# Layer 1's state-space scan in units of 32 channels by 4 states: shared delta and delta*u tiles, B and C spread by TensorE, the product with C in place

## The chip, the cores and the metric

The kernel runs on one core of one Trainium2 chip. The metric is the device time of one execution in microseconds (us); lower is better. Three runs of the kernel before gave 7250.67, 7251.33 and 7258.51 us, median 7251.33 us.

## What is computed

Four layers run in sequence on an image tensor of 4 x 96 channels x 64 x 64, in float32. Layer 0 is two Mamba blocks over the 4096 tokens of each image. Layer 1, which the change is about, is two 2-D selective scans ("ss2d", a and b). Layers 2 and 3 (a spectral block, quantized feed-forwards, linear attention) are untouched. The core of layer 1, for each image and each of four directions k (rows, columns, and both backwards), with d = 96 channels, N = 8 states, L = 4096 tokens:

```
x_dbl = jnp.einsum('bkdl,kcd->bkcl', xs, xproj_w)
dts = jnp.einsum('bkrl,kdr->bkdl', x_dbl[:, :, :R], dt_w)
Bs = x_dbl[:, :, R:R + N]
Cs = x_dbl[:, :, R + N:]
A = -jnp.exp(A_logs).reshape(K, d, N)
delta = jax.nn.softplus(dts + dt_b[None, :, :, None])
dA = jnp.exp(delta[..., None] * A[None, :, :, None, :])
dBu = delta[..., None] * jnp.transpose(Bs, (0, 1, 3, 2))[:, :, None] * xs[..., None]
...
h = a * h + bu
return (h, jnp.einsum('bkdn,bkn->bkd', h, c))
```

Around the scan stand a 3x3 depthwise convolution with Silu in front, a gate branch Silu(z), and behind it a sum of the four directions, a layer norm, the gate and an output projection.

## The kernel before

Three stages follow each other: `stage_mamba` (layer 0), `stage_ss2d` (layer 1) and `stage_tokens` (layers 2 and 3). Within a stage nothing is issued directly: each operation is recorded by `Plan.add`, and `Plan.order` (L388) then lists all of them engine by engine, by costs that it assumes for each kind of operation, the order of recording breaking ties. So every instruction of a stage carries line 474 in the profile, and rows are told apart by tile names. The five engines' queues run in that order, each waiting for what its next instruction needs; all DMAs are issued by SyncE (SP), in order. `Plan(close_first=True)` (layer 0 only) makes the plan finish a "mm" tile of PSUM that it has opened before it opens another.

**Layer 1.** There are 8 blocks (4 images, a and b). A block has 16 **turns**: 4 directions (two forwards, two backwards) by 4 tiles of T = 1024 tokens. `Tokens.prepare` makes delta (96 rows; 16 more rows of the same matmul hold B and C), writes both to DRAM (`dd`), multiplies delta by the input on POOL (`du`) and writes 32 of its 96 rows to DRAM (`ud`). `narrow` reads the 8 rows of C back, splits them into three bf16 parts (`split_steps`) and stacks them (`bc_stack`, 24 rows). `mix` makes the turn's table `bc`: B is spread over the 128 partitions by a DMA, C by two bf16 matmuls and two ScalarE copies.

A turn has 6 **units** of 16 channels by 8 states on 128 partitions (`Scan`, L589). For each unit, at its step s:

- `load` (5 units ahead): a 512 KB DMA spreads 16 rows of delta over 128 partitions (`sc_d`).
- `decay` (2 ahead): ScalarE makes exp(A * delta).
- the input term delta*u*B. In 4 units of 6 ("spread"), `inputs` has TensorE spread delta*u into PSUM (`s<-du,c_sel`, two float32 matmuls) and `scan` has VectorE multiply it there by B. In the other 2, a 512 KB DMA spreads `ud` (`sc_u`) and POOL multiplies it by B; the decay is then in PSUM.
- `scan`: VectorE's `tensor_tensor_scan` over 1024 tokens, backwards through a reversed view where the direction is backwards; ScalarE keeps the last column (`carry`) for the next turn.
- `outputs`: POOL multiplies the states by C into a new tile `sc_h`.
- `reduce`, after each round of three units: TensorE sums over the states into `y` in PSUM (`y<-sc_h,c_red`), and `end` adds that to `ysum` on VectorE after two rounds.

`plan` (L1510) interleaves the next turns' `prepare`, `narrow` and `mix`, and over a whole block the work for its neighbours: the next block's convolution (`mm<-xp,w_conv`, 9 float32 matmuls for each 512 tokens) and gates, and the previous block's `finish`.

**Layer 0** already has the form that the change gives to layer 1 (`QuadScan`, L755): units of 32 channels by 4 states, so that one `sc_d` and one `sc_u` tile serve several units; TensorE spreads B from the bf16 stack into PSUM (`s<-bc_stack,selb`); VectorE multiplies that by `sc_u`; POOL multiplies the states `sc_h` by C into a second tile `sc_y`. Both layers have 768 units.

Of the kernel before, what the change touches and what calls it, by code (L numbers as in the profile page):

```python
# [11 lines left out]
F32 = mybir.dt.float32  # L12
# [21 lines left out]
def in_psum(index):  # L34

    return index % 3 != 2


def shape_constants():
# [12 lines left out]
    red = np.zeros((128, 32), f)  # L52
    red[p, p // QS] = 1.0
    out["c_red0"] = red
    red = np.zeros((128, 2, 32), f)
    for r in range(2):
        red[p, r, r * 16 + p // NS1] = 1.0
    out["c_red1"] = red
    at = np.arange(3 * NS0) % NS0
    sel = [at[:, None] == QS * q + p % QS for q in range(NS0 // QS)]  # L60
    out["c_selb0"] = np.stack(sel, 1).astype(f)
    out["c_selbc"] = (np.arange(3 * NS1)[:, None] % NS1 == p % NS1).astype(f)
    sel = np.zeros((C, C // 16, 128), f)
    for j in range(C // 16):
        sel[j * 16 + p // NS1, j, p] = 1.0
    out["c_sel1"] = sel
# [28 lines left out]
def arrange(w):  # L95
# [36 lines left out]
    def blocks(a):  # L132
# [30 lines left out]
        [w[q + "A_logs" + x].reshape(NDIR, C * NS1 // 128, 128) for x in s], 0  # L163
    ).transpose(3, 0, 1, 2)
# [400 lines left out]
class Turn:  # L565
# [4 lines left out]
    def in_psum(self, index):  # L570
        return in_psum(index)

    def begin(self, q, yps):

        return False


class Unit:


    def __init__(self, turn, q, r, j, index, rows):
        self.turn, self.q, self.r, self.j, self.index, self.rows = turn, q, r, j, index, rows
        self.spread = turn.in_psum(index)
        self.first = index == 0
        self.round = []
        self.last = False


class Scan:  # L589

    LOOK = 5

    def __init__(self, k, rep, ps, n_state, red, bufs):
        self.k = k  # L600
        self.rep, self.ps, self.red, self.bufs = rep, ps, red, bufs
        self.ns, self.dl = n_state, 128 // n_state
        self.per = 32 // self.dl
        self.yps = None

    @property
    def nc(self):
        return self.k.nc

    def spread_states(self, src):  # L610

        return bass.AP(src.tensor, src.offset, [(T, self.ns), (0, self.dl), (1, T)])

    def spread_channels(self, src, j):

        at = src.offset + j * self.dl * T
        if self.ns == NS0:
            return bass.AP(src.tensor, at, [(0, self.ns), (T, self.dl), (1, T)])
        return bass.AP(src.tensor, at, [(T, self.dl), (0, self.ns), (1, T)])

    def units(self, turn, parts):


        out = []
        for q, groups in enumerate(parts):
            for r in range(self.per):
                new = []
                for g, rows in groups:
                    new.append(Unit(turn, q, r, g * self.per + r, len(out) + len(new), rows))
                    new[-1].round = new  # L630
                out += new
            out[-1].last = True
        return out

    def load(self, u):
        nc = self.nc
        u.d = self.rep.tile([128, T], F32, tag="sc_d", name="sc_d", bufs=self.bufs[0])
        nc.sync.dma_start(out=u.d, in_=self.spread_channels(u.turn.dd, u.j))
        if not u.spread:
            u.u = self.rep.tile([128, T], F32, tag="sc_u", name="sc_u", bufs=self.bufs[1])  # L640
            nc.sync.dma_start(out=u.u, in_=self.spread_channels(u.turn.ud, u.j))

    def decay(self, u):
        if not u.spread:
            u.s = self.ps.tile([128, T], F32, tag="s", name="s_ps", bufs=2)
            self.nc.scalar.activation(u.s, u.d, AF.Exp, scale=u.turn.acol(u.j))
        else:
            self.nc.scalar.activation(u.d, u.d, AF.Exp, scale=u.turn.acol(u.j))

    def inputs(self, u):  # L650
        u.s = self.ps.tile([128, T], F32, tag="s", name="s_ps", bufs=2)
        with self.nc.side_by_side(overlap=25.0 if self.halves(u) else 0.0):
            for h, (table, du) in enumerate(u.turn.spread(u)):
                self.nc.tensor.matmul(u.s[:, h * W:(h + 1) * W], table, du, start=True, stop=True)

    def halves(self, u):

        return u.turn.spread(u)[0][1].ap[0][1] <= 64

    def scan(self, u):  # L660
        nc = self.nc
        init, keep = u.turn.carries(u.j)
        if not u.spread:
            a, b, u.h = u.s, u.u, u.u
        else:
            a, b, u.h = u.d, u.s, u.d
            nc.vector.tensor_tensor(b, b, u.turn.bc[:, 0, :], ALU.mult)
        if u.turn.rev:
            nc.vector.tensor_tensor_scan(u.h[:, ::-1], a[:, ::-1], b[:, ::-1], init, ALU.mult, ALU.add)
        else:  # L670
            nc.vector.tensor_tensor_scan(u.h, a, b, init, ALU.mult, ALU.add)
        if keep is not None:
            nc.scalar.copy(keep, u.h[:, 0:1] if u.turn.rev else u.h[:, T - 1:T])

    def outputs(self, u):
        u.c = self.rep.tile([128, T], F32, tag="sc_h", name="sc_h", bufs=self.bufs[2])
        self.nc.gpsimd.tensor_tensor(u.c, u.h, u.turn.bc[:, 1, :], ALU.mult)

    def reduce(self, us):

        nc = self.nc
        r = us[0].r
        held = True
        if r == 0:
            self.yps = self.ps.tile([128, T], F32, tag="y", name="y_ps", bufs=1)
            held = us[0].turn.begin(us[0].q, self.yps)
        halves = [[h] for h in range(T // W)] if len(us) > 2 else [range(T // W)]
        for hs in halves:
            with nc.side_by_side():
                for h in hs:  # L690
                    for u in us:
                        row, col, at = u.rows[h]
                        nc.tensor.matmul(
                            self.yps[row:row + 32, col:col + W], self.red[:, r, :], u.c[:, at:at + W],
                            start=not held, stop=r == self.per - 1, skip_group_check=True,
                        )

    def run(self, units, plan):


        nc = self.nc
        works = []
        for s in range(-self.LOOK, len(units) + 5):
            def at(n):
                return units[n] if 0 <= n < len(units) else None

            works += plan(s)
            u = at(s + self.LOOK)
            if u:
                if u.first:  # L710
                    u.turn.ready.finish()
                self.load(u)
            for w in works:
                w.pace(s)
            works = [w for w in works if not w.done]
            u = at(s - 3)
            if u and u is u.round[-1]:
                self.reduce(u.round)
            u = at(s - 4)
            if u and u.last:  # L720
                u.turn.end(u.q, self.yps)
            u = at(s + 2)
            if u and u.spread:
                self.decay(u)
            u = at(s)
            if u:
                self.scan(u)
            u = at(s + 2)
            if u:
                if not u.spread:  # L730
                    self.decay(u)
                else:
                    self.inputs(u)
            if u and not u.spread:
                nc.gpsimd.tensor_tensor(u.u, u.u, u.turn.bc[:, 0, :], ALU.mult)
            u = at(s)
            if u:
                self.outputs(u)
        for w in works:
            w.finish()  # L740


class Quad:
# [11 lines left out]
class QuadScan:  # L755
# [4 lines left out]

    LOOK = 4

    def __init__(self, k, rep, ps, red, selb, bufs, y):
        self.k = k
        self.rep, self.ps, self.red, self.selb, self.bufs, self.y = rep, ps, red, selb, bufs, y
        self.yps = None
# [5 lines left out]
    def units(self, turn, parts):  # L772
# [3 lines left out]
        for m, (rows, rounds) in enumerate(parts):  # L776
            for r, those in enumerate(rounds):
                new = []
                for g, q, pooled in those:
                    new.append(Quad(turn, m, g, q, pooled, len(out) + len(new), rows[g]))  # L780
                    new[-1].round, new[-1].place = new, (r, len(rounds))
                out += new
            out[-1].last = True
# [18 lines left out]

    def load(self, u):
        def fill(tag, bufs, src):
            t = self.rep.tile([128, T], F32, tag=tag, name=tag, bufs=bufs)
            self.nc.sync.dma_start(out=t, in_=src)
            return t
# [63 lines left out]
    def run(self, units, plan):  # L871
# [4 lines left out]
        for s in range(-self.LOOK, len(units) + 5):  # L876
# [9 lines left out]
            for w in works:  # L886
                w.pace(s)
# [1040 lines left out]
```

## Time and profile before

One execution was profiled: 7245.79 us, of which the span from the first to the last instruction is 7243.7 us. "Busy" is the time in which an engine has an instruction at work.

| | span of 7243.7 us | layer 0, 104 to 2790 us | layer 1, 2850 to 6062 us |
|---|---|---|---|
| length, us | 7243.7 | 2686 | 3212 |
| PE (TensorE) busy, us | 6069.7 | 2164.0 | 2793.8 |
| DVE (VectorE) busy, us | 5862.6 | 2513.7 | 2708.2 |
| ACT (ScalarE) busy, us | 4424.7 | 1567.3 | 2269.8 |
| POOL (GpSimd) busy, us | 5855.0 | 2530.9 | 2821.8 |
| mean busy share of the 16 DMA engines | 0.60 | 0.42 | 0.91 |
| granted TensorE clock | 0.865 | 0.81 | 0.92 |

A busy share near 1 does not by itself name the bound: an engine that is in step with another has to wait for it now and then, and what a stage can gain is read from the idle time of its busiest engine and from what that idle time waited for.

### The profile page before, as it was taken

The page shows a single profiled execution, that of the slowest core. Times are in us where ns is not written, and L with a number is a line of the kernel's source. Part 1 is how long each engine was busy: PE and PEld are TensorE (multiplying, and loading weights), DVE is VectorE, ACT ScalarE, POOL GpSimd, SP SyncE. Part 2 cuts the span into 40 slices and gives each one's busy share as a digit, 9 for nine tenths or more (in the row PEclk, how much of TensorE's full clock was granted, in tenths as well). Part 3 has the DMA queues.
Part 4 walks back from the last instruction along what each step waited for, and adds up shares of the span by engine and source line. Part 5 has one row for each costly group of instructions (what it writes and reads, how often), then busy time and mean ns, then how long its engine had stood idle before and what let it go on. Part 6 is the DMA issues. An engine that isn't in the chain of part 4 may idle for free. (4 is left out here: it accounts for less than half of the span.)

```text
span 7243.7 us, 79973 instructions
## 1 busy us (share of the span) xinstructions
PE 6069.7 (84%) x26408; PEld 2258.7 (31%) x26408; DVE 5862.6 (81%) x4659; ACT 4424.7 (61%) x6590; POOL 5855.0 (81%) x2994
## 2 busy tenths in 40 slices
PE   7888888888888876888989888899989786888987
PEld 2222222222222212223233222333233223655555
DVE  5999999999999995888888888878888895355464
ACT  5565556556666554776767667676867673445444
POOL 5999999999999995889898888889898895234344
PEclk8888878887888877989999888899999897798888
DMA  4344444444444444999899988889999995011210
GB/s 144 130 144 135 137 133 145 153 137 136 139 144 133 145 141 123 236 229 232 221 239 231 234 226 226 230 226 238 237 235 229 229 259 157 19 33 45 47 29 19
DMA packets 447841, 1181.40 MB, mean 163 GB/s; under 512 B 120490, under 2 KB 133923, under 8 KB 445888
## 3 DMA queue, kind: packets, MB, share of 16 engines
q1 hardware_dynamic: 447424, 1176.29, 59.6%
q8 instruction: 207, 3.39, 0.2%
q14 instruction: 210, 1.72, 0.1%
HBM read 998.47 MB, written 177.41 MB: 162 GB/s over the span
## 5 line engine op out<-in xcount | busy, mean ns | idle before, releaser
L474 POOL TENSOR_TENSOR sc_y<-sc_h,sc_c 128x1024 f32<-128x1024 f32 x768 | 1795.6, 2354 | 125.7 <-DVE sc_h L474 106.6
L474 POOL TENSOR_TENSOR sc_h<-sc_d,bc 128x1024 f32<-128x1024 f32 x512 | 1199.5, 2357 | 135.0 <-ACT bc L474 90.5
L474 PE MATMUL s<-du,c_sel 96*128 96x512 f32 x2048 | 1093.0, 663 | 208.9 <-DVE sc_d L474 147.3
L474 DVE TENSOR_TENSOR_SCAN sc_d<-sc_d,carry,s 128x1024 f32<-128x1024 f32 x384 | 899.3, 2343 | 57.2 <-ACT sc_d L474 34.2
L474 PE MATMUL y<-sc_y,c_red 128*32 128x512 f32 x3072 | 747.1, 745 | 206.9 <-POOL sc_y L474 206.7
L474 DVE TENSOR_TENSOR_SCAN sc_h<-sc_h,carry,s 128x1024 f32<-128x1024 f32 x384 | 900.7, 2346 | 19.6
L474 DVE TENSOR_TENSOR s<-s,bc 128x1024 f32<-128x1024 f32 x512 | 623.9, 1219 | 218.6 <-PE s L474 195.1
L474 ACT ACTIVATE sc_h<-sc_d,w_alog 128x1024 f32<-128x1024 f32 x512 | 584.3, 1144 | 331.6 <-POOL sc_y L474 330.3
L474 ACT ACTIVATE sc_d<-sc_d,w_alog 128x1024 f32<-128x1024 f32 x512 | 584.7, 1146 | 158.0 <-DMA sc_d<-dd 155.8
L474 DVE TENSOR_TENSOR s<-s,sc_u 128x1024 f32<-128x1024 f32 x512 | 621.5, 1214 | 71.6 <-PE s L474 70.9
L474 POOL TENSOR_TENSOR sc_h<-sc_u,bc 128x1024 f32<-128x1024 f32 x256 | 602.9, 2355 | 84.5 <-PE y L474 64.1
L474 PE MATMUL y<-sc_h,c_red 128*32 128x512 f32 x3072 | 623.7, 649 | 53.3 <-POOL sc_h L474 48.0
L474 POOL TENSOR_TENSOR sc_u<-sc_u,bc 128x1024 f32<-128x1024 f32 x256 | 603.9, 2359 | 64.3 <-DMA sc_u<-ud 48.9
L474 PEld LDWEIGHTS s<-du,c_sel 96*128 96x128 f32 x2048 | 392.4, 205 | 823.3 <-issue 395.5
L474 ACT ACT_TABLE_LOAD x493 | 632.5, 1283 | 22.4 <-issue 9.9
L474 ACT ACTIVATE s<-sc_d,w_alog 128x1024 f32<-128x1024 f32 x512 | 570.2, 1114 | 108.9 <-DVE sc_d L474 50.8
L474 POOL TENSOR_TENSOR ln_rs<-ln_rs_e,mhalf 128x4 f32<-128x4 f32 (+1 forms) x224 | 253.3, 1133 | 457.8 <-DMA ln_rs_e<-ln_sq 220.8
L474 POOL TENSOR_TENSOR sc_h<-sc_u,sc_b 128x1024 f32<-128x1024 f32 x256 | 602.2, 2352 | 20.5 <-POOL sc_y L474 2.6
L474 PE MATMUL s<-bc_stack,selb 48*128 48x512 bf16 x1024 | 372.6, 454 | 262.8 <-DVE sc_h L474 254.6
L474 PE MATMUL mm<-xp,w_conv 96*96 96x512 f32 x1152 | 541.4, 609 | 4.3 <-ACT ysum L474 1.7
L474 DVE TENSOR_TENSOR_SCAN sc_u<-s,carry,sc_u 128x1024 f32<-128x1024 f32 x192 | 448.4, 2335 | 45.8 <-POOL sc_u L474 36.8
L474 DVE TENSOR_TENSOR_SCAN sc_h<-s,carry,sc_h 128x1024 f32<-128x1024 f32 x192 | 447.6, 2331 | 8.9 <-ACT s L474 4.9
(215 smaller groups left out, 10243.7 us busy)
## 6 DMA issues: line engine op xcount, KB each, us to landing
sc_d<-dd SPq DMA_DIRECT2D x960, 512.0 KB
sc_u<-ud SPq DMA_DIRECT2D x448, 512.0 KB
sc_c<-bcd SPq DMA_DIRECT2D x128, 512.0 KB
bc<-dd SPq DMA_DIRECT2D x128, 512.0 KB
dd<-delta SPq DMA_DIRECT2D x128, 448.0 KB
sc_b<-bcd SPq DMA_DIRECT2D x64, 512.0 KB
dd<-delta SPq DMA_DIRECT2D x64, 384.0 KB
ud<-du SPq DMA_DIRECT2D x64, 384.0 KB
```

The source lines that it names most:

```text
L474: getattr(getattr(self.nc, op.engine), method)(*a, **kw)
```

## The change

In layer 1 the class `Scan` gives way to `QuadScan`, which is renamed `Scan` (and `Quad` becomes `Unit`); layer 0 runs on the same class. In detail:

- A turn still has 6 units, now 3 groups of 32 channels by 2 sets of 4 states. One `sc_d` and one `sc_u` tile per group serve two units each. Two units of six are "pooled" (POOL makes the input term, with B from a DMA, `sc_b`); for the other four TensorE spreads B from the stack and VectorE multiplies by `sc_u`.
- `narrow` takes B and C (16 rows, so that its tiles have 128 rows and the stack 48). `mix` is gone: the C tables of both sets of states (`sc_c`) are made in the new `table`, three units ahead, by two bf16 matmuls and two ScalarE copies each. All 96 rows of `ud` go to DRAM, and `du` has one buffer instead of two.
- `outputs`, in both layers, writes POOL's product over the states that it reads: the tile has 1025 columns, and the product lies one column before the states (one behind in backward directions, where POOL now walks all three operands backwards). Layer 0's `sc_y` goes; `sc_h` has 10 buffers there, 8 in layer 1.
- Layer 1's plan gets `close_first=True`; loads stand four units ahead instead of five; layer 0's C loads stand three units ahead instead of four.

```diff
+    LOOK, TABLES = 4, 3
...
+    def table(self, u):
+        if not u.brings_c:
+            return
+        if u.q not in self.made:
+            u.turn.cs[u.q] = self.fill("sc_c", self.bufs[3], self.states(u.turn.cd, u.q))
+            return
+        c = u.turn.cs[u.q] = self.rep.tile([128, T], F32, tag="sc_c", name="sc_c", bufs=self.bufs[3])
+        for at in range(0, T, W):
+            pc = self.ps.tile([128, W], F32, tag="mm", name="c_ps")
+            self.nc.tensor.matmul(
+                pc, self.selb[:, self.made[u.q], :], u.turn.stack[:, at:at + W], start=True, stop=True
+            )
+            self.nc.scalar.copy(c[:, at:at + W], pc)
 
     def decay(self, u):
-        u.h = self.rep.tile([128, T], F32, tag="sc_h", name="sc_h", bufs=self.bufs[4])
+        tile = self.rep.tile([128, T + 1], F32, tag="sc_h", name="sc_h", bufs=self.bufs[4])
+        u.h, u.c = tile[:, 1:T + 1], tile[:, 0:T]
+        if u.turn.rev:
+            u.h, u.c = u.c, u.h
...
     def outputs(self, u):
-        u.c = self.rep.tile([128, T], F32, tag="sc_y", name="sc_y", bufs=self.bufs[5])
-        self.nc.gpsimd.tensor_tensor(u.c, u.h, u.turn.cs[u.q], ALU.mult)
+        out, h, c = u.c, u.h, u.turn.cs[u.q]
+        if u.turn.rev:
+            out, h, c = (v[:, ::-1] for v in (out, h, c))
+        self.nc.gpsimd.tensor_tensor(out, h, c, ALU.mult)
...
+            u = at(s + self.TABLES)
+            if u:
+                self.table(u)
...
-    sc = QuadScan(k, rep, ps, k.load(wp, "c_red0"), selb, (4, 4, 2, 5, 5, 5), (W, 2))
+    sc = Scan(k, rep, ps, k.load(wp, "c_red"), selb, (4, 4, 2, 5, 10), (W, 2))
...
-    pl = Plan(nc)
+    pl = Plan(nc, close_first=True)
...
-    sc = Scan(k, rep, ps, NS1, k.load(wp, "c_red1"), (6, 2, 5))
+    selb = wp.tile([3 * 2 * NS1, 4, 128], BF16, name="selb")
+    sc = Scan(k, rep, ps, k.load(wp, "c_red"), selb, (4, 4, 2, 3, 8), (T, 1), {0: 2, 1: 3})
...
-            du = wk.tile([C, T], F32, tag="du", name="du", bufs=2)
+            du = wk.tile([C, T], F32, tag="du", name="du", bufs=1)
...
-            nc.sync.dma_start(out=ud[64:C, :], in_=du[64:C, :])
-            self.dd, self.du, self.ud = dd, du, ud
+            nc.sync.dma_start(out=ud, in_=du)
+            self.dd, self.ud = dd, ud
+            self.bd, self.cd = dd[C:C + NS1, :], dd[C + NS1:CD, :]
 
         def narrow(self):
 
-            x = wk.tile([64, 128], F32, tag="bc_in", name="bc_in", bufs=1)
-            part = [(128, 8), (T, NS1), (1, 128)]
-            at = self.dd[C + NS1:CD, :]
-            nc.sync.dma_start(out=x, in_=bass.AP(at.tensor, at.offset, part))
+            x = wk.tile([128, 128], F32, tag="bc_in", name="bc_in", bufs=1)
+            part = [(128, 8), (T, 2 * NS1), (1, 128)]
+            nc.sync.dma_start(out=x, in_=bass.AP(self.bd.tensor, self.bd.offset, part))
...
-        def mix(self):
-
-            self.bc = wk.tile([128, 2, T], F32, tag="bc", name="bc")
-            src = self.dd[C:C + NS1, :]
-            nc.sync.dma_start(
-                out=self.bc[:, 0, :], in_=bass.AP(src.tensor, src.offset, [(0, 16), (T, NS1), (1, T)])
-            )
-            yield
-            for at in range(0, T, W):
-                pb = ps.tile([128, W], F32, tag="mm", name="bc_ps")
-                nc.tensor.matmul(pb, selbc, self.stack[:, at:at + W], start=True, stop=True)
-                nc.scalar.copy(self.bc[:, 1, at:at + W], pb)
-                yield
...
-    groups = [(g, ((32 * g, 0, 0), (32 * g, W, W))) for g in range(3)]
-    units = [u for turn in turns for u in sc.units(turn, (groups,))]
-    size, slot = NCH, NCH * NDIR * NT
+    tiles = {g: ((32 * g, 0, 0), (32 * g, W, W)) for g in range(3)}
+    rounds = (((0, 0, False), (1, 1, True), (2, 0, False)), ((1, 0, False), (0, 1, True), (2, 1, False)))
+    units = [u for turn in turns for u in sc.units(turn, [(tiles, rounds)])]
+    size = len(units) // len(turns)
+    slot = size * NDIR * NT
...
-        if at == 3 and 1 <= n + 1 < len(turns):
-            turns[n + 1].mixed.due = s + 3
-            out.append(turns[n + 1].mixed)
```

## The prediction

> **What bounds the kernel now.** I read the page's 40 slices first: DMA stands at 4 tenths in layer 0, at 9 in layer 1, near 1 behind. Then the busy times by window: layer 0, layer 1, and stretches inside layer 1.
>
> ```profile
> 104.00:2790.00 2686.00, 2163.96 (x8438) 579.68 (x8436) 2513.65 (x1649) 1567.33 (x2223) 2530.88 (x1139) 0.81 0.42 136
> 2850.00:6062.00 3212.00, 2793.77 (x8252) 958.50 (x8252) 2708.20 (x1833) 2269.75 (x3387) 2821.84 (x1283) 0.92 0.91 230
> 3450.00:3550.00 100.00, 98.31 (x277) 33.32 (x278) 84.21 (x55) 74.13 (x106) 87.33 (x38) 0.97 0.95 231
> 3550.00:3650.00 100.00, 79.50 (x207) 23.10 (x202) 81.12 (x51) 78.18 (x111) 78.07 (x34) 0.86 0.81 219
> 5850.00:5950.00 100.00, 80.34 (x265) 27.62 (x264) 94.11 (x68) 74.59 (x112) 99.49 (x48) 0.97 1.01 259
> 5722.00:6062.00 340.00, 265.83 (x818) 86.86 (x817) 307.75 (x211) 220.40 (x337) 322.02 (x147) 0.93 0.92 235
> ```
>
> Columns: window and length, busy us of PE, PEld, DVE, ACT, POOL, then granted clock, DMA share, GB/s. The reader is to see this. In layer 0 POOL is busy 2530.88 / 2686 = 94.2% of the time and DVE 93.6%: these two in step are the bound. In layer 1 POOL has 87.9%, DVE 84.3%, PE 87.0%, DMA 91%: four resources near full, none full. In 3450 to 3550 the next block's convolution runs, PE is full (98.3) and POOL falls to 87.3. In 5850 to 5950, in the last block, there is no next convolution: PE needs 80.3 and POOL reaches 99.5, although DMA is at 1.01. So POOL is the floor of layer 1, and PE's surplus work pushes the stage above it. By blocks: the last one begins near 5707, 15 us (four units) ahead of its first row of `ysum<-xc,dsum,y` at 5722, and takes 355 us; the seven before it take (5707 - 2890) / 7 = 402 us each.
>
> The waits in layer 1 then say what the floor waits for:
>
> ```profile
> POOL sc_h L474 <- ACT bc L474: 90.5, 25, 12.7
> POOL sc_h L474 <- PE y L474: 66.0, 26, 8.5
> POOL sc_u L474 <- DMA sc_u<-ud: 48.9, 10, 24.8
> ...
> DVE s L474 <- PE s L474: 195.1, 137, 4.4
> DVE bc_in L474 <- ACT mm L474: 106.0, 49, 25.8
> ```
>
> (us, times, longest.) POOL idles 3212 - 2822 = 390 us: for the C table, for PE's reduction that frees its output tiles, for `sc_u`. DVE's longest wait is for PE's spread.
>
> **The change, part by part.** Rows used:
>
> ```profile
> L474 PE MATMUL s<-du,c_sel 96*128 96x512 f32 x2048 | 1093.0, 663 | 208.9 <-DVE sc_d L474 147.3
> L474 POOL TENSOR_TENSOR sc_h<-sc_d,bc 128x1024 f32<-128x1024 f32 x512 | 1199.5, 2357 | 135.0 <-ACT bc L474 90.5
> L474 POOL TENSOR_TENSOR sc_u<-sc_u,bc 128x1024 f32<-128x1024 f32 x256 | 603.9, 2359 | 64.3 <-DMA sc_u<-ud 48.9
> L474 DVE TENSOR_TENSOR s<-s,bc 128x1024 f32<-128x1024 f32 x512 | 623.9, 1219 | 218.6 <-PE s L474 195.1
> L474 PE MATMUL s<-bc_stack,selb 48*128 48x512 bf16 x1024 | 372.6, 454 | 262.8 <-DVE sc_h L474 254.6
> ```
>
> *PE.* The float32 spreads go: 1093.0 us. Layer 0's bf16 spread of the same shape comes, 1024 matmuls for 372.6. The C tables double: layer 1's group of 256 matmuls `mm<-bc_stack,selbc` was busy 98.0 us, so 512 cost 196. Sum: 2793.8 - 1093.0 + 372.6 + 98.0 = 2171 us. Layer 0, PE less full, got clock 0.81 against 0.92; at that clock it is 2171 x 0.92 / 0.81 = 2466 us, still under POOL's floor. [...]
>
> *POOL.* The same 768 products, 256 input terms and 128 `du` as now, at 2.357 us: 2822 us, unchanged. Two things about the 768 products are in no row: input and output one column apart in one tile, and, in the 384 of backward turns, a step of minus one. Working in place is free by the rows (`sc_u<-sc_u,bc` 2359 ns against 2357 for a new tile). For the offset, PE's taps over `hn` (column offsets 0 to 3) and its fixed-offset read both have median 592 to 593 ns. For the step, the nearest row by access is DVE's scan, forward and backward in one group of 384: 2310 / 2347 / 2350 ns (least, median, most), so no cost; the far end is a large stride, `xt<-xc` on ACT 1985 ns against 1057 for 96x1024 in a row, x1.88, which would be 384 x 0.88 x 2.357 = 796 us on POOL. A gain has no reason. I take 0, the row with the same step, and keep 796 as the other end. [...]
>
> *DVE.* The same scans, the same 512 products (layer 0's form with `sc_u`: 1214 ns against 1219): 2708 us.
>
> *ACT.* 256 table copies of 577 ns become 512: +148 us, to 2418. The narrowing works on 128 rows instead of 64, in instructions that layer 0 shows in the same group at 278 to 307 ns: nothing.
>
> *DMA.* Per layer 1: 384 fewer `sc_d` and 128 more `sc_u` of 512 KB (-134 MB), `ud` 256 KB more x128 (+34), narrowing 64 to 128 KB or so more x128 (+17): 740 to about 656 MB. By the share of now, 0.91 x 3212 x 656 / 740 = 2590 us. SP issues 256 fewer of the large loads; each wait in SP's order holds back all DMAs behind it, as now.
>
> *Waits added.* The four spreads of a turn and both C tables need `bc_stack`; before, the C table alone did, and the spreads took `du` from SBUF. The stack of turn n+2 is recorded near the start of turn n+1; the first spread is recorded 2 units ahead of its turn. Between lie about three units, some 11 to 12 us, for three writes, one read and the last split. Behind a late spread on PE stand the reductions, which free `sc_h`, and DVE's product. POOL's product now ends the life of no tile: `sc_h` lives from the decay to the reduction, 7 units at most by the recorded order, of 8 buffers. `ud` covers all loads of `sc_u`, four units ahead; `du`'s one buffer waits for the last write, a turn earlier. The C copies wait for a buffer three tables back, out of use for about a turn.
>
> *Layer 0.* The same instructions in the same numbers; POOL and DVE set its pace. More buffers for `sc_h` let ACT's decays run earlier (they idled 330 us for POOL's products), off the path. C loads three units ahead, near 10 us: cover enough. 0, at either side +-10.
>
> *The plan's order* (`close_first`) has no row: layer 0 runs with it at 94.2%. 0, and inside the range.
>
> **The sum.** POOL's floor is 2822 us, and what changes is the share that it reaches. With PE at 2171 instead of 2794 and less DMA, the rows with PE not full apply: 94.2% in layer 0, 322.02 / 340 = 94.7% in the last block. I take 93.5%, a little under both, since ACT will be at 2418 / 3018 = 80% (58% in layer 0, 65% in the last block) and the lull of 3550 to 3650 (Silu's table loads and gates, POOL 78) is not touched. 2822 / 0.935 = 3018, that is -194 us. Against the profiled execution: 7245.8 - 194 = 7052, rounded to **7050 us**. That execution stands 5.5 us below the median of the runs shown, and the sum isn't finer than that. Its own range: at 90.5%, 3118, or 7152; at 97.7%, the mean of the windows of the last block from 5650 to 5950 (97.8, 95.7, 99.5), 2888, or 6922.
>
> **Rivals.**
>
> *A late stack eats the gain.* Spreads and tables stall in order at each turn's start, with ACT fuller. For it: DVE already waits 106 us for the narrowing on ACT, up to 25.8 at once, and POOL 90.5 for a C table. Against: PE waited only 22.8 us for the stack. At 1 us per turn, 128 of 194 is gone: 7180; band 7152 to 7231.
>
> *The freed PE was no limit.* POOL's idle time is the latencies of ACT and DMA, which remain, and the change is neutral: 7246. Against it: the last block, where only the block work is missing, is 47 us shorter.
>
> *Backward POOL products cost more* (ends slower). Place: 384 products of directions 2 and 3. They take the stage past its present length when 2822 + 384 x > 0.935 x 3212 = 3003, at x = 0.47 us each, +20%. At half the far end, 398 us: 3220 / 0.935 = 3444, +232, or 7478; at the whole of it 3618 / 0.935 = 3870, or 7904. For it: no row of POOL reads backwards. Against: DVE's scan.
>
> **How the numbers follow.** Forecast (6922 to 7152) 0.65; late stack 0.17; neutral 0.04; backward products 0.13; better than the forecast's range 0.01. 0.2% is about what a measurement of this kernel can tell from no change: 14.5 us. Faster 0.65 + 0.17 + 0.01 = 0.83, same 0.04, slower 0.13. The range takes the forecast's own and the nearer half of the late stack, 6930 to 7200; left out are the slower cases, neutral and the far half of the late stack, about 0.2.
>
> **What would show it.** Right: layer 1 near 3020 us, POOL products at 2.36 us in both directions, POOL 93 to 94%, no float32 spread, PE near 2200 to 2450 us, DMA share about 0.86, blocks with convolution near the last block's length. Wrong: POOL products in two durations; PE or ACT waiting on `bc_stack` by more than 100 us; layer 0's 2686 us moved by more than 10; a clock near 0.5.

## The result: 7290.5 us, 0.42% slower

Five runs of the changed kernel gave 7286.09 to 7320.33 us, median 7290.52; the kernel before, on the same chip, 7250.67 to 7273.78, median 7258.51. The ratio is 1.0042, 95% interval 1.0022 to 1.0062: slower, outside the range of the prediction. The profiled execution took 7293.38 us, its span 7291.6. The experiments ran on five chips, on which the kernel before had medians of 7283 to 7292 us. So times are compared only as ratios to the kernel before on the same chip (the change itself has 1.0042), and lengths inside the traces.

Two lengths are read from every trace below: the end of layer 0 (start of the last `sz<-y,sz`), and layer 1 from GpSimd's fill of `xp` to the start of the last `ysum<-ysum,y`. Before: 2783.6 and 3268 us. After: 2817.4 and 3275 us. So layer 0, forecast at 0 +-10, lost 34 us; layer 1, forecast at -194, lost 8. Where one program of layer 1 ran in two kernels, its lengths differed by 7 (3275, 3282) and 17 us (3252, 3235): differences under about 20 us are not read. A length is of one execution, a ratio is of medians over 4 to 28, and the untouched rest behind layer 1 took 1182 us in the trace of the kernel before and 1188 to 1233 in the others. Lengths and ratios can therefore differ by some 30 us; where it matters, both are given.

### The profile page after: what moved, and what is told of

Same layout as the page of the kernel before. It is cut to its first block, busy times and chain, and to the rows that moved or that the text cites. A ratio compares the mean times of both kernels' runs of the same rounds, so it can differ in the third digit from the quotient of the medians.

```text
span 7291.6 us, 77456 instructions
## 1 busy us (share of the span) xinstructions
PE 5758.9 (79%) x25640; PEld 2026.7 (28%) x25640; DVE 5876.0 (81%) x4659; ACT 4542.0 (62%) x6848; POOL 5855.0 (80%) x2994
## 5 line engine op out<-in xcount | busy, mean ns | idle before, releaser
L458 POOL TENSOR_TENSOR sc_h<-sc_h,sc_c 128x1024 f32<-128x1024 f32 x1536 | 3595.4, 2356 | 333.3 <-DVE sc_h L458 270.4
L458 DVE TENSOR_TENSOR_SCAN sc_h<-sc_h,carry,s 128x1024 f32<-128x1024 f32 x768 | 1802.0, 2347 | 34.0 <-ACT sc_h L458 0.6
L458 PE MATMUL y<-sc_h,c_red 128*32 128x512 f32 x6144 | 1510.0, 797 | 219.9 <-POOL sc_h L458 132.5
L458 ACT ACTIVATE sc_h<-sc_d,w_alog 128x1024 f32<-128x1024 f32 x1024 | 1163.7, 1147 | 625.4 <-PE y L458 533.3
L458 DVE TENSOR_TENSOR s<-s,sc_u 128x1024 f32<-128x1024 f32 x1024 | 1246.7, 1218 | 321.4 <-PE s L458 319.9
L458 POOL TENSOR_TENSOR sc_h<-sc_u,sc_b 128x1024 f32<-128x1024 f32 x512 | 1211.1, 2366 | 181.9 <-PE y L458 114.3
L458 PE MATMUL s<-bc_stack,selb 48*128 48x512 bf16 x2048 | 748.8, 457 | 742.3 <-DVE sc_h L458 725.6
L458 DVE TENSOR_TENSOR_SCAN sc_h<-s,carry,sc_h 128x1024 f32<-128x1024 f32 x384 | 896.3, 2334 | 42.6 <-ACT s L458 31.2
L458 DVE TENSOR_TENSOR_SCAN sc_h<-sc_h,s 128x1024 f32<-128x1024 f32 x256 | 585.4, 2287 | 10.2
L458 PE MATMUL mm<-hn,conv_w 97*64 97x512 f32 x1536 | 362.3, 614 | 0.2 <-ACT sz L458 0.2
L458 PE MATMUL mm<-bc_stack,selb 48*128 48x512 bf16 x512 | 202.0, 441 | 125.2 <-DMA bc_stack<-bsd 48.7
```

The source lines that it names most:

```text
L458: getattr(getattr(self.nc, op.engine), method)(*a, **kw)
```

## The profile after

Busy times by window of the kernel after (length, busy us of PE, PEld, DVE, ACT, POOL, then granted clock, DMA share, GB/s): layer 0, layer 1 (the same stretch as before, though the stage now starts 34 us later), its second block, which has a convolution, and its last.

```profile
104.00:2790.00 2686.00, 2060.18 (x8378) 578.05 (x8375) 2492.02 (x1633) 1552.21 (x2216) 2504.10 (x1129) 0.80 0.41 136
2850.00:6062.00 3212.00, 2552.95 (x7476) 724.03 (x7476) 2695.19 (x1830) 2404.50 (x3657) 2806.38 (x1280) 0.78 0.62 206
3354.00:3744.00 390.00, 318.83 (x972) 93.96 (x972) 334.29 (x224) 306.67 (x463) 352.19 (x160) 0.80 0.62 207
5758.00:6098.00 340.00, 235.90 (x691) 58.06 (x690) 306.97 (x207) 217.94 (x344) 310.22 (x143) 0.67 0.57 194
```

POOL, DVE and ACT have the work that was forecast. PE's busy time fell by 241 us, where the work taken from it would have been some 620 us at the old clock (an estimate: 2794 - 2171, the prediction's sum): the clock went from 0.92 to 0.78. POOL reaches 2806 / 3212 = 87.4%, as before (87.9), not 93.5.

Groups of PE in layer 1, 2890 to 6050 us, before (first fence; the float32 spread of 1093 us is left out) and after. Behind the bar stand busy us and mean ns; matmuls overlap, so the busy time is less than count times mean (first row: 3060 x 647 ns are 1980 us, busy 617):

```profile
L474 PE MATMUL y<-sc_h,c_red 128*32 128x512 f32 x3060 | 617.1, 647 | 48.4 <-POOL sc_h L474 43.1 <-DVE ysum L474 4.9
L474 PE MATMUL mm<-xp,w_conv 96*96 96x512 f32 x1054 | 496.1, 608 | 2.5 <-ACT bc L474 1.5 <-DVE ysum L474 0.7
```

```profile
L458 PE MATMUL y<-sc_h,c_red 128*32 128x512 f32 x3012 | 826.5, 819 | 158.6 <-DVE ysum L458 80.7 <-POOL sc_h L458 74.0 <-POOL du L458 3.4
L458 PE MATMUL mm<-xp,w_conv 96*96 96x512 f32 x1098 | 511.7, 622 | 30.3 <-ACT sc_c L458 29.4 <-ACT delta L458 0.5
L458 PE MATMUL s<-bc_stack,selb 48*128 48x512 bf16 x1008 | 363.4, 452 | 204.0 <-DVE sc_h L458 200.6 <-ACT bc_part L458 3.0
```

The reduction `y` is the same instruction in both, and takes 819 ns instead of 647: 209 us more of busy time. The convolution, nine matmuls on end, nearly keeps its time (608, 622).

Waits of layer 1 in the kernel after, 2890 to 6100 us (us, times, longest):

```profile
POOL sc_h L458 <- DVE sc_h L458: 166.6, 135, 5.2
POOL sc_h L458 <- PE y L458: 44.2, 25, 4.1
POOL sc_h L458 <- ACT sc_c L458: 39.0, 10, 9.9
...
DVE s L458 <- PE s L458: 227.4, 120, 8.0
DVE bc_in L458 <- ACT mm L458: 91.9, 62, 25.5
...
ACT sc_h L458 <- PE y L458: 166.0, 93, 7.0
...
PE mm L458 <- ACT sc_c L458: 129.4, 135, 8.8
...
PE mm L458 <- DMA bc_stack<-bsd: 48.7, 18, 6.9
```

The float32 spread is gone, and DVE waits longer for spreads than before (195.1). Splitting DVE's idle time ahead of its products by what PE executed in it: before 218 us, 173 of them the float32 spread and 31 the convolution; after 228 us, 72 the bf16 spread and 117 the convolution. POOL now waits for DVE's scans.

## The experiments

In what follows "the rule" is `close_first`, and "the relief" is bf16 spreads in place of float32 ones. Theories at the start: *tile life* (in place, a state's tile is freed only by PE's reduction); *TensorE* (the freed time went back by the lower clock, or into its queue, where the convolution stands ahead of spreads); *C tables* (their doubled work ate the gain); *order* (the rule `close_first`, or the plan's assumed costs).

### Layer 0 and the order

**e1_sep0.** The state and its product with C get separate tiles in layer 0, as before:

```
-    sc = Scan(k, rep, ps, k.load(wp, "c_red"), selb, (4, 4, 2, 5, 10), (W, 2))
+    sc = Scan(k, rep, ps, k.load(wp, "c_red"), selb, (4, 4, 2, 5, 5, 5), (W, 2))
...   (with six numbers: sc_h 5 buffers, and sc_y 5 for the product)
```

> Layer 0 alone goes back to two tiles per unit (5 buffers for the states, 5 for the products, nothing written in place); layer 1 stays as changed. Theory 'tile life': written in place, a layer 0 tile comes free only when TensorE has reduced it, so the decays and POOL's input terms wait for TensorE (POOL waited 71 us for y in layer 0, before 4 us); then layer 0 ends some 34 us earlier again (last product near 2782 us instead of 2815) and the whole is near 7257. Rival 'order': the loss comes from the C loads one unit later or from the shifted operands; those with the C loads stay here, so the whole would stay near 7290.

Ratio 0.9996 (0.9980 to 1.0012); layer 0 ends at 2788.4. Layer 0's waits, before, after, and in this kernel:

```profile
POOL sc_y L474 <- PE y L474: 4.0, 5, 2.2
```

```profile
POOL sc_h L458 <- DVE sc_h L458: 99.7, 109, 2.8
POOL sc_h L458 <- PE y L458: 71.0, 65, 4.3
...
ACT sc_h L458 <- PE y L458: 367.2, 180, 6.9
```

```profile
POOL sc_y L458 <- PE y L458: 3.7, 5, 2.2
...
ACT sc_h L458 <- POOL sc_y L458: 328.8, 179, 6.1
```

In place, POOL's input term takes a tile that waits for PE's reduction (71 us); in its own tile, a state is free as soon as POOL has read it. 29 of the 34 us are this; the other 5 lie within the spread, so the C loads, which stay one unit later in e1, are not the cause.

**e2_cdma.** The C tables of layer 1 come by DMA, so PE and ACT lose them:

```
-    {0: 2, 1: 3}   (C tables made by TensorE)
+                   (filled by DMA from dd)
```

> The C tables of layer 1 come by DMA (two loads of 512 KB per turn) instead of TensorE and ScalarE. Theory 'C tables': the table matmuls stand in TensorE's queue waiting for ScalarE's copies (129 us) with spreads behind them, and ScalarE has 148 us more work than before the change; layer 1 gets 60 to 150 us shorter, the whole 7140 to 7230. Rival 'clock or tile life': layer 1 stays within 20 us of what it is, since DMA has room (share 0.62) and the limit lies elsewhere.

Ratio 1.0162 (1.0141 to 1.0183), layer 1 3375 us: 100 longer, with PE at 2406 and ACT at 2115 busy us in the window of 3212. As it stands the theory falls. But e10 below, which drops a table with no DMA in its place, gains, so the tables do cost; the 100 us come with the loads: whether by their traffic or by their place in SP's order was not told apart.

**e3_noclose.** Layer 1's plan without `close_first`:

```
-    pl = Plan(nc, close_first=True)
+    pl = Plan(nc)
```

> Layer 1's plan without close_first, as before the change. Theory 'order': finishing opened mm tiles first holds back spreads and reductions in TensorE's queue; the whole gets at least 20 us shorter. Rivals: within 20 us, or longer, as the C tables fill the mm ring more.

Ratio 1.0209 (1.0184 to 1.0234), layer 1 3402 us. So the rule is worth 126 us in the changed kernel, and the theory falls. Without it C tables come late from the two shared tiles:

```profile
POOL sc_h L458 <- ACT sc_c L458: 100.6, 28, 13.8
POOL ysum L458 <- ACT ysum L458: 77.9, 33, 6.2
...
ACT sc_c L458 <- PE mm L458: 160.4, 161, 7.3
```

**e4_dup.** Layer 1's spreads are issued twice:

```
+                for _ in range(2 if self.made else 1):
                     self.nc.tensor.matmul(u.s[:, at:at + W], ...)
```

> In layer 1 each spread of B is computed twice into the same tile (1024 more bf16 matmuls, near 370 us of TensorE time; the values are the same). Theory 'TensorE still limits' (the clock gave back what was freed): layer 1 gets longer by 60 us or more. Rival 'TensorE is no limit any more': within 20 us, the granted clock goes up from 0.78 and takes up the added work.

Ratio 1.0173 (1.0153 to 1.0194), layer 1 3387 us:

```profile
2850.00:6062.00 3212.00, 2704.27 (x8253) 812.74 (x8254) 2602.32 (x1769) 2337.34 (x3543) 2710.65 (x1237) 0.78 0.61 199
```

More work on PE still costs (112 us), though PE is no fuller than before the change, and the clock does not rise with it (0.78 in both). The doubled spread also lengthens the step that DVE waits for (227 us of such waits became 316), so PE's load and the latency of a spread were not told apart.

### What in layer 1 costs, one part at a time

**e5_tap1.** One of nine taps:

```
-                for tap in range(9):
+                for tap in (4,):
```

> The changed kernel whose convolution does one of its nine taps (it leaves out the other eight, in every block of layer 1: 7 of 8 blocks have theirs inside the scan). It takes 8 of 9 matmuls of 8.4 us per convolution tile off TensorE and nothing off the other engines. Layer 1 takes 3275 us in the changed kernel. Theory 'convolution ahead of spreads': 117 of VectorE's 228 us of idle time before its products is convolution, so layer 1 is at least 117 us shorter (below 3160), and the seven blocks with a convolution come within 20 us of the last one's length (345 us against 396, 390, 396, 426, 414, 395, 382). Rival 'the convolution is not what limits' (tile life, or the narrowing on ScalarE): layer 1 loses less than 60 us, and the blocks stay above 380 us.

Ratio 0.9946 (0.9926 to 0.9966), layer 1 3216 us: 60 shorter, on the rival's edge. The blocks with a convolution stay at 381 to 411 us, the last one at 341. The clock sinks again, from 0.78 to 0.70, and busy time falls by 218 us only:

```profile
2850.00:6062.00 3212.00, 2334.63 (x6562) 598.17 (x6562) 2731.26 (x1855) 2414.79 (x3678) 2837.51 (x1297) 0.70 0.63 206
```

**e6_exempt.** The rule spares the convolution:

```
-                    if self.close_first:
+                    if self.close_first and len(h.ops) < self.close_first:
...
+    pl = Plan(nc, close_first=10)   (layer 1; 1000 in layer 0, where the rule stays as it was)
```

> The changed kernel, in whose layer 1 the rule that closes an open shared tile first is not applied to the convolution's tile of nine matmuls and a copy; the tiles of the narrowing and of the C tables keep it. Only the order changes. Theory 'convolution ahead of spreads' (the nine taps stand in one piece ahead of spreads that VectorE waits for): layer 1 is at least 50 us shorter than the changed kernel's 3275, and VectorE's 228 us of idle time before its products falls below 150. Rival 'ring of shared tiles': a convolution that is spread out holds one of the ring's buffers longer, C tables wait for it as they do without the rule, and layer 1 is longer, up to the 3402 us without the rule.

Ratio 1.0015 (0.9997 to 1.0033), layer 1 3278. DVE's idle time over a convolution fell from 117 to 47 us, but idle over spreads, reductions and copies grew, 205 in all. The convolution's place is not the cause either.

**e7_sep1.** Separate tiles in layer 1:

```
-    sc = Scan(k, rep, ps, k.load(wp, "c_red"), selb, (4, 4, 2, 3, 8), (T, 1), {0: 2, 1: 3})
+    sc = Scan(k, rep, ps, k.load(wp, "c_red"), selb, (4, 4, 1, 3, 4, 5), (T, 1), {0: 2, 1: 3})
...   (sc_h 4 buffers, sc_y 5, sc_b 1)
```

> The changed kernel, in whose layer 1 GpSimd's product with C goes to a tile of its own (five buffers) and the state's tile has four buffers, as in the kernel before; for room sc_b has one buffer instead of two. Theory 'tile life' (in place, a state's tile is freed only by TensorE's reduction): the waits of ScalarE's decays (166 us) on TensorE's reduction in layer 1 go, and layer 1 is at least 30 us shorter than 3275. Rival 'TensorE's time limits layer 1 whatever holds the tiles': the wait moves to GpSimd's product, whose output tile TensorE frees (66 us in the kernel before), and layer 1 stays within 20 us, or is longer where the single sc_b is missed.

Ratio 1.0138 (1.0119 to 1.0157), layer 1 3368: longer by 93. The waits of ACT's decays on the reduction are gone from the list's head, and others have come:

```profile
POOL sc_y L458 <- DVE sc_h L458: 204.9, 143, 4.5
...
DVE s L458 <- PE s L458: 267.1, 126, 7.4
...
ACT sc_c L458 <- PE mm L458: 155.8, 132, 4.8
```

The gain that the theory asked for is not there. How much of the 93 us is the single `sc_b` was not told apart, so tile life in layer 1 is not ruled out.

**e8_cost.** The plan at PE's costs of the lower clock:

```
+    pl.per = (2.15, 0.72)           (layer 1; ns per column, was 1.68, 0.42)
-            with nc.side_by_side():
+            with nc.side_by_side(overlap=200.0 if self.made else 25.0):
```

> The changed kernel, in whose layer 1 the planner reckons TensorE's matmuls at the lower granted clock: 2.15 ns per column in float32 instead of 1.68, 0.72 in bf16 instead of 0.42, and 200 ns instead of 25 for each further matmul of a reduction. Only the order changes. Theory 'plan's costs' (the plan believes that TensorE has time left, and orders spreads and tables too late): layer 1 is at least 50 us shorter than 3275. Rival 'order is not the cause': within 20 us, or longer.

Ratio 0.9975 (0.9964 to 0.9987), layer 1 3252: 23 shorter by the length, 49 by the ratios (0.9975 against 1.0042), between the theories. Order alone, with the same work, moves the stage.

**e10_onec.** One C table for both state groups:

```
+        if u.turn.cs:
+            u.turn.cs[u.q] = u.turn.cs[0]
+            return
```

> The changed kernel without the second C table in layer 1: both state groups are multiplied with the first one (it leaves out the values of the second). It takes 256 matmuls of 0.44 us off TensorE, 256 copies of 0.58 us (149 us) off ScalarE and 256 uses of the ring of two shared tiles. Theory 'doubled C tables ate the gain': layer 1 at least 80 us shorter than the changed kernel's 3275. Rival 'they cost nothing that shows': within 30 us.

Ratio 0.9943 (0.9924 to 0.9962), layer 1 3231: 44 shorter by the length, some 70 by the ratios (0.9943 against 1.0042), between theory and rival. The second table costs, by the length half of what its theory said.

### The premise by itself

**e9_freed, e13_close, e18_relief.** The kernel before with relief and rule (e9), with the rule alone (e13) and with the relief alone (e18). The relief leaves out the right values: rows of the stack stand in for `du`.

```
-        return [(sel[:, u.j, :], self.du[:, h * W:(h + 1) * W]) for h in range(2)]
+        return [(selbc, self.stack[:, h * W:(h + 1) * W]) for h in range(2)]   (e9, e18)
-        with self.nc.side_by_side(overlap=25.0 if self.halves(u) else 0.0):
+        with self.nc.side_by_side(overlap=0.0):                                   (e9, e18)
-    pl = Plan(nc)
+    pl = Plan(nc, close_first=True)                                            (e9, e13)
```

> The kernel before, with TensorE's relief alone: in layer 1 the 2048 float32 spreads of du (663 ns each) become bf16 matmuls of 48 rows from the stack (454 ns), under the rule that closes an open shared tile first. Units, tiles, loads and the single C table stay as before. (It leaves out the right values: the stack's rows stand in for du.) It takes about 0.35 us off each of the 2048 matmuls at the clock of before. Theory of the prediction (PE's surplus pushes layer 1 above POOL's floor): layer 1 at or under 3080 us, 190 less than the kernel before's 3268. Theory 'TensorE's time was not what held POOL back', drawn from the blocks (POOL is busy 90% in the first seven of both kernels, and has 33 us less work in the last one): within 60 us of 3268, with a lower granted clock than 0.92.

> The kernel before with nothing but the ordering rule (an open shared tile is closed first) in its layer 1. It is the part of e9 that is not TensorE's relief. Theory 'the relief gives the 43 us of e9': layer 1 within 15 us of the kernel before's 3268. Rival 'the rule gave them': 3225 to 3240, and the relief alone nothing.

> The kernel before with TensorE's relief alone and without the ordering rule in layer 1: the 2048 float32 spreads of du become bf16 matmuls of 48 rows from the stack (it leaves out the right values: the stack's rows stand in for du). With the rule the relief took layer 1 from 3352 to 3224 us. Theory 'the two add': the relief is worth 128 us without the rule too, layer 1 about 3140. Rival 'the relief acts only with the rule' (in the changed kernel the rule was worth 126 us): layer 1 at 3268 or longer, up to 3350.

(The stack of the kernel before has 24 rows, not 48; a spread took 463 to 467 ns.)

| layer 1, us | without the rule | with it |
|---|---|---|
| float32 spreads | 3268 (before) | 3352 (e13), ratio 1.0076 (1.0059 to 1.0092) |
| bf16 spreads | 3258 (e18), ratio 0.9982 (0.9964 to 0.9999) | 3224 (e9), ratio 0.9961 (0.9943 to 0.9980) |

This is the answer to the forecast. Units, loads, tables and order rule as before, PE relieved of the float32 spreads: 10 us by the length, 13 by the ratio (1 to 26), not 194. Layer 1's window in e18, and its reduction:

```profile
2850.00:6062.00 3212.00, 2501.36 (x7243) 716.16 (x7242) 2704.54 (x1833) 2278.41 (x3397) 2821.28 (x1283) 0.77 0.91 231
```

```profile
L474 PE MATMUL y<-sc_h,c_red 128*32 128x512 f32 x3062 | 787.3, 798 | 42.8 <-POOL sc_h L474 26.1 <-DVE ysum L474 16.3
```

Clocked work is busy time times granted clock: PE's went from 2794 x 0.92 = 2570 to 2501 x 0.77 = 1926 us. At the old clock 1926 would be 1926 / 0.92 = 2093 busy us, an estimate: by it, of the 701 us that were freed, 408 went back to the clock. The other 293 us left PE less busy, and POOL, with the same 2821 us of work, took 3258 us for it in place of 3268. Its waits moved. In the kernel before (first fence, 2890 to 6050 us) it waited 90.5 us for C tables and 66.0 for reductions; in e18 it waits for DVE's scans, and DVE for spreads as long as before (195.1):

```profile
POOL sc_h L474 <- DVE sc_d L474: 23.8, 24, 2.5
```

```profile
POOL sc_h L474 <- DVE sc_d L474: 108.9, 92, 9.0
POOL sc_h L474 <- ACT bc L474: 52.9, 20, 10.1
...
POOL sc_h L474 <- PE y L474: 10.3, 10, 1.8
...
DVE s L474 <- PE s L474: 189.3, 93, 23.5
...
PE s L474 <- DVE sc_u L474: 143.4, 92, 4.7
PE s L474 <- DVE sc_d L474: 133.3, 74, 8.1
```

The last two rows are PE waiting until DVE's scans free a tile of `s`: DVE and PE wait for each other (PE 277 us in these two, 197 in the kernel before).

The rule alone makes layer 1 of the kernel before 85 us longer (55 by the ratio). DVE waits longer for spreads, and of its idle time ahead of its products 93 us (31 before) lay over convolutions and 214 (173) over float32 spreads:

```profile
DVE s L474 <- PE s L474: 315.9, 157, 8.5
```

With bf16 spreads it makes layer 1 33 us shorter (15 by the ratios). Neither e13's theory (nothing) nor its rival (a gain), and neither of e18's (3140; 3268 and over): relief and rule act together, by 118 us by the lengths and 70 by the ratios. That the two need each other is shown; the size is not settled.

The account of layer 1 then runs, by lengths in us: 3268, rule 3352, relief 3224 (e9), the change with one C table 3231 (e10), with both 3275. The relief's 128 us go to the rule's 85 and the second table's 44; units, shared tiles and in-place products together cost 7, within the spread. By the ratios, with layer 0's part taken off, the same four steps are about +55, -84, -40 and +70: the same end and other sizes. On one chip e10 had a median of 7250 us against e9's 7261 with a layer 0 that is 31 us longer. So whether the new units gain nothing or some 40 us stays open.

### What holds POOL at 88%

**e11_nob, e14_noprod, e15_neither.** The changed kernel without input multiplications, on POOL (e11), on VectorE (e14), on both (e15):

```
-            a, b = u.s, u.h                                                 (e11, e15)
+            a, b = u.s, u.turn.inputs[u.g] if self.made else u.h
...
-                    nc.gpsimd.tensor_tensor(u.h, u.turn.inputs[u.g], u.turn.bs[u.q], ALU.mult)
+                    if self.made:
+                        pass   (else as before)                             (e11, e15)
...
+            if not self.made:                                               (e14, e15)
                 nc.vector.tensor_tensor(b, b, u.turn.inputs[u.g], ALU.mult)
```

> The changed kernel without GpSimd's 256 input products in layer 1: VectorE's scan reads the spread delta*u as it is loaded (it leaves out the multiplication with B in a third of the units). 256 x 2.36 = 604 us of GpSimd's 2822 us of work in layer 1 go; VectorE keeps its 2708, the others theirs. Theory 'GpSimd's work is the floor, reached to 90% in the blocks': layer 1 falls until VectorE's work takes its place, 2708 / 0.90 plus some 90 us at the head: 3100, at least 150 us less than 3275. Rival 'latencies between the engines set the pace, no engine's work': less than 60 us shorter.

> The changed kernel without VectorE's 512 products of spread B and delta*u in layer 1: the scan reads the spread B as it is (it leaves out the multiplication by delta*u in two thirds of the units). 512 x 1.22 = 624 us of VectorE's 2708 us go, GpSimd keeps its 2822. Theory 'VectorE's work in step with TensorE holds GpSimd back': GpSimd then comes near its own work, 97% in the blocks: 2822 / 0.97 plus some 110 us at the head, 3020, about 250 less than 3275. Rival 'GpSimd's own work and its other waits are the bound': less than 100 us shorter, as with the cut on GpSimd.

> Both cuts together: layer 1 without GpSimd's 256 input products and without VectorE's 512 products (both multiplications that make a scan's input are left out). Left are VectorE 2084 us, GpSimd 2218, ScalarE 2418, TensorE 2553 at the clock of now. Theory 'GpSimd and VectorE in step are the bound, and TensorE is close behind': about 2800 us, TensorE or ScalarE over 85%, the clock above 0.78 since TensorE's work is packed tighter. Rival 'the order of the engines' work, whatever its amount': over 3000.

**e16_neither_tap1, e17_neither_dvec.** From e15, one convolution tap (e16), or the C copies on VectorE (e17):

```
+                for tap in (4,):                                            (e16)
+            self.nc.vector.tensor_copy(c[:, at:at + W], pc)                 (e17)
```

> The kernel without both input multiplications in layer 1 (e15: layer 1 3144 us), whose convolution does one tap of nine (it leaves out the other eight too). TensorE loses about 450 us of its 2606 busy us, the others nothing. Theory 'TensorE at its granted clock is the bound': layer 1 at least 200 us shorter than 3144. Rival 'ScalarE': less than 60 us, and TensorE's clock sinks from 0.78 towards 0.70.

> The kernel without both input multiplications in layer 1 (e15: layer 1 3144 us), in which VectorE, by then busy 70%, makes the 512 copies of the C tables in layer 1 that ScalarE made (297 us of ScalarE's 2437). TensorE has the same work. Theory 'ScalarE is the bound': layer 1 at least 150 us shorter than 3144. Rival 'TensorE at its granted clock': less than 60 us.

(Their 3144 counts to the end of the last sum; by the measure used here e15 is 3142.)

| kernel | work cut in layer 1 | layer 1, us | shorter by | ratio |
|---|---|---|---|---|
| e11 | POOL 604 us | 3182 | 94 | 0.9901 (0.9870 to 0.9933) |
| e14 | DVE 624 us | 3210 | 65 | 0.9915 (0.9892 to 0.9938) |
| e15 | both, 1228 us | 3142 | 134 | 0.9833 (0.9818 to 0.9848) |
| e16 | and PE's 8 taps, some 455 us | 3040 | 102 more | 0.9715 (0.9694 to 0.9735) |
| e17 | and ACT 297 us (to DVE) | 3083 | 58 more | 0.9761 (0.9745 to 0.9778) |

POOL and DVE in e11, and layer 1's window of e15:

```profile
POOL sc_h L458 <- DVE sc_h L458: 583.2, 332, 10.8
...
DVE s L458 <- PE s L458: 189.5, 111, 6.6
```

```profile
2890.00:5900.00 3010.00, 2463.74 (x7335) 722.93 (x7334) 2051.96 (x1295) 2358.48 (x3589) 2184.20 (x1007) 0.79 0.65 215
```

e11's 94 us lie between its theory and its rival; e14 and e15 end on their rivals' side. POOL's work alone is not the floor: relieved by a fifth, it waits for DVE's scans (583 us). DVE's is not either. With both far from full (72.6% and 68.2%), layer 1 is 4% shorter. PE's cut gives 102 us, between e16's two theories, while the clock goes from 0.79 to 0.71; ACT's gives 58, just inside e17's rival. Each cut in the table returned a tenth to a quarter of the work taken away. So no single engine's amount of work sets layer 1's time. What is left is the chain between them: two `s` buffers and two shared tiles passed round four queues, in the order that the plan chose. That is argued from the rest: no run had more buffers there, and which link is worth most stays open. Nor did any run hold the order still: each edit of the work lets the plan list everything anew, and order alone moved layer 1 by 23 us (e8) and 126 us (e3).

### A version that beats both

**e12_best.** The edits of e1 and e8 together.

> The changed kernel with the two edits that helped: separate tiles for the state and its product with C in layer 0, as before, and layer 1's planner at TensorE's costs of the lower clock. Layer 0 got 29 us shorter by the first, layer 1 21 us by the second. If the two add: 50 us under the changed kernel, a ratio of 0.993 to the kernel before. If the second was chance in the order: 0.996 to 1.0.

As forecast if the two edits add: median 7247.45 us, ratio 0.9943 (0.9924 to 0.9962): 0.6% faster than the kernel before and, by the ratios, 1% faster than the change as made. Layer 0 ends at 2790.2, layer 1 takes 3235.

## Why the prediction was wrong, point by point

- **PE's work: right; its clock: too high.** 2171 us x 0.92 = 1997 of clocked work was forecast, 2553 x 0.78 = 1991 came. At layer 0's 0.81 it would have been 2466 us by the prediction's estimate, at 0.78 it is 2553.
- **POOL's share: the step that failed.** "With PE at 2171 instead of 2794 and less DMA, the rows with PE not full apply": POOL was to go from 87.9% to 93.5% once PE was no longer full. It stayed at 87.4%. e18 takes PE's surplus away alone: 644 us of clocked work less, and the stage is 10 us shorter, not 194. (The order of the queues is new in it too, since the plan lists by costs.)
- **What misled: the last block.** It was read as the same POOL work without PE's surplus, 47 us faster. A block of the middle before:

```profile
3304.00:3696.00 392.00, 348.88 (x1050) 120.71 (x1049) 334.97 (x225) 281.88 (x424) 350.73 (x161) 0.93 0.91 230
```

  POOL has 351 us of work here and 322 in the last block: 29 of the 52 us between the two lengths are POOL's own work, for the neighbouring blocks. In the middle POOL stood at 89.5% already. The window of 3212 us begins 76 us ahead of the first block (2926), and POOL has 35 us of work in them, so 2822 us in a stage of 3018 asked for (2822 - 35) / (3018 - 76) = 94.7% in every block, the last block's own share. And with eight of nine taps of the convolution gone (e5) the middle blocks kept their 381 to 411 us: what the last block lacks is not only the convolution on PE.
- **ACT, DVE, POOL, bytes: right.** 2405 us against 2418, 2695 against 2708, 2806 against 2822; 206 GB/s x 3212 us = 662 MB against 656. The DMA share, forecast 0.86 from the bytes, is 0.62. What that buys alone no run shows: e9, at a share of 0.91, is 7 us shorter than e10, at 0.63, by the length, and some 40 longer by the times.
- **The second table: not hidden.** Its 148 us on ACT and 98 on PE were put inside the 93.5%; it costs 44 us by the length, some 70 by the ratios (e10).
- **`close_first`: 0 was wrong both ways**, +85 us alone (55 by the ratio), -126 in the changed kernel.
- **Layer 0: +34, not 0.** "More buffers for `sc_h` let ACT's decays run earlier": ten buffers of longer life are worth 29 us less than five and five (e1).
- **Products with C: right**, at 0. Forward and backward, shifted, in place, from the tile's own view (least, median, most, ns):

```profile
L458 POOL TENSOR_TENSOR sc_h<-sc_h,sc_c x1536: 2325/2354/2428, 94.6 to 6097.3; 128x1024 f32<-128x1024 f32 x192
```

  The most is 2.43 us, so the rival with a price of 0.47 us or more on 384 of them falls.
- **The late stack: not it.** PE waited 48.7 us for `bc_stack`, 26 more than before.
- **The neutral rival**, given 0.04, said that POOL's idle time is latency of ACT and DMA, which remains. Its number held in layer 1, its reason only in part: POOL's longest wait is now for DVE's scans (166.6 us). Layer 0 made the rest of the loss.

## What to carry to other kernels

Before a stage is said to be held by one engine's surplus, take that engine's work away alone and look: here 644 us of clocked work off a busy engine gave 10. A window that seems to show a stage without the surplus must be compared in the floor engine's own busy time, not in length alone. And an in-place product saves memory but lengthens the life of its tile to the next reader's end (in layer 0 POOL waited 71.0 us for PE's reduction with products in place, 3.7 us with separate tiles): count buffers times life.

## What the runs showed of the hardware

In these runs TensorE's granted clock was mostly lower where it had less work: in layer 1 0.92 before, 0.78 after, 0.70 in e5. The reduction `y` in layer 1, before and after (least, median, most, ns):

```profile
L474 PE MATMUL y<-sc_h,c_red x3060: 589/592/1063, 2910.8 to 6049.5; 128*32 128x512 f32 x192
```

```profile
L458 PE MATMUL y<-sc_h,c_red x3012: 590/640/1063, 2940.0 to 6046.3; 128*32 128x512 f32 x189
```

This one instruction has mostly two durations, near 592 and near 1060 ns, 1.8 apart; 41 of 3072 lay between 700 and 1000 ns before, 139 after. Counted over layer 1, 297 of 3072 took 1000 ns or more before, 1403 after; in e18 the mean is 798 ns, against 647 and 819. The prediction read the clock of a PE less full off layer 0, at 0.81. There 891 of 3072 reductions took 1000 ns or more before the change, 29%; in layer 1 after it, at 0.78, 46%. The clock of layer 1 went with PE's clocked work per us: 0.80 before at 0.92, 0.62 after at 0.78, 0.51 in e5 at 0.70, and PE's busy share stayed between 0.73 and 0.87. It did not follow it always: e4, at 0.66, kept 0.78.
